# Late layernorms on VectorE, masks made ahead of layer 1, walk products ahead of the searches

## The chip, the cores and the metric

The kernel runs on one core of a Trainium2 chip. The metric is the device time of one execution in microseconds, as a median of several. The engines that matter are TensorE (PE in the profile: matrix products and transposes, into PSUM), VectorE (DVE), ScalarE (ACT), GpSimd (POOL) and the DMA queues; SyncE (SP) issues most of the transfers.

## What is computed

2708 nodes with 256 features go through two layers, each with a residual and a layernorm. All data is f32.

```
# layer 0, x: (2708, 256)
R = adj + I;  R = R / R.sum(-1)
Xf = Xa = x;  Z = 0
for n in range(2):
    A  = top_p_attention(Xa)      # softmax rows; the largest entries that make up 0.9, renormalised
    Xf = R @ Xf                   # the walk
    Xa = A @ Xa                   # the attention
    Z  = Z + Xf @ U1[n].T + Xa @ U2[n].T
x = layernorm(x + layernorm(x + Z) * ln_g + ln_b)
# layer 1, 4 heads of 64
Wh  = x @ W[h];  s_i, s_j = the two halves of a[h] with Wh
e   = leaky_relu(s_i + s_j, 0.2), masked by adj != 0 and the diagonal
out = layernorm(x + softmax_j(e) @ Wh)
```

## The kernel before

**Tiles.** The nodes are 22 row tiles, 16 of 128 rows and 6 of 110. Of PE, ACT, DVE and POOL each executes its instructions in the order in which the program is written (a manual schedule); so a line that stands earlier in the program goes earlier on each of its engines. Only SP's transfers are ordered by a scheduler.

**Layer 0** (fast_layer0) has two steps. In each step, row tile t needs a *search*, a *walk* and an *attention*. The search (L842) computes the row's scores on PE (the groups named lg, L661), exponentials on ACT (e, L665), tallies on ACT (junk, L686), and on DVE a bound (L751), the candidates (max8, L766), sorting and settling (L784 to L832) and the final masked row with its sum (L835). The attention turns e on PE (tr, L240), copies it to SBUF on ACT (eT, L245) and multiplies (att, L258); at its end ACT writes xa (L1030). The walk (walks, L855) is a stream of products, 22 a tile, of blocks of adj with the features; its PSUM tile has one buffer (ps_wk). When a tile's walk ends, DVE adds the tile itself (xf, L915, in step 0; xw, L974, in step 1), and only then may the next tile's walk begin.

A *slot* (L999) interleaves these. It advances the searches that are going by one part, may begin a new one, advances the work that finishes tiles, and then takes some walk products from the stream:

```
def slot(spend, begin=None):
    advance(going)
    if begin and begin[1] < NT:
        going.append(search(*begin)); next(going[-1])
    advance(doing)
    owed[0] += spend
    while owed[0] > 0:
        ...
```

Between the two steps there is no attention to interleave with: 15 slots of 7 walk products each run the first three searches of step 1 (L1117 to L1121). Within step 1, slots spend 6 or 7 products (SPEND_1).

**The end of layer 0.** finish (L969) adds up a tile, normalises it twice (norms, L181, layernorm on DVE with one power on POOL) and computes its *sources* (L156): two transposes of xe into PSUM (L160), a copy on ACT, two products with the layer's weights (L166), and from these the exponentials sb and tj and the values v, stored to DRAM. The last LATE = 4 tiles stop before the normalisation; their sums stay in x_late and they are normalised within layer 1.

**Layer 1** (L1193). The rows i are taken in three groups of 8, 8 and 6 tiles; for a group all 22 blocks j of neighbours are added up in PSUM. For block j the *mask* (neighbours, L1214) is loaded by SP into one of three buffers (blk) and turned to 0 and 1 by two passes of ACT, Sign and Square (L1221, L1222); where the block holds the diagonal DVE sets it (L1225). With the mask comes the load of v (L1290) in the first group, issued by ACT. The *weights* pt (L1302) are four operations of DVE, one a head: the larger of r and tj, times the mask. PE multiplies the *values* (L1313, 16 products a block) and the *denominators* (L1323, 16 a block). pt has three blocks' buffers (DEEP = 3). The main loop (from L1369) takes blocks in pairs: both blocks' values, then both blocks' denominators, then weights and masks of the blocks ahead. Twice a pair it calls *beside* (L1344), which advances other work by one part: the four late tiles (prepared, L1330) in group 0, the verdict (L1126; some 20 small operations of DVE that check that the searches held, and one product), and the settling of the group before (L1228).

prepared uses layernorm_beside (L138): ACT sums x (L145), POOL makes the mean (L146), ACT sums the squares (L148), POOL makes the variance, the power and the offset (L149 to L151), ACT writes the result (L153), and POOL multiplies by ln_g and adds x (L187, L188) between the two layernorms. The sources of the four late tiles are the last blocks of group 0.

**The tail** (from L1406). After the last group its six tiles are settled: PE transposes, DVE takes the reciprocal (L1236), ACT scales each head (L1247, even tiles) or DVE does all at once (L1242, odd tiles), POOL adds xe (L1252), DVE makes the statistics, POOL the power and the offset (L1262, L1263), ACT writes o (L1265; two buffers) and SP stores it.

Of the kernel before, what the change touches and what calls it, by code (L numbers as in the profile page):

```python
# [8 lines left out]
F32 = mybir.dt.float32  # L9
# [35 lines left out]
def kernel(  # L45
# [68 lines left out]
    g_sb = const.tile([P, D], F32, name="g_sb")  # L114
    b_sb = const.tile([P, D], F32, name="b_sb")

    LATE = 4
    x_late = const.tile([P, LATE, D], F32, name="x_late")
    engines = {nc.tensor.engine, nc.scalar.engine, nc.vector.engine, nc.gpsimd.engine}

# [57 lines left out]
            )  # L178
        queue.dma_start(vd[t][:m], vt[:m])  # L179

    def norms(t, xt, norm=layernorm, other=None):  # L181

        m = rows[t]
        hh = xe[:m, t, 0:D]
        h2 = hh if other is None else other()[:m]
        yield from norm(h2, hh, m)
        nc.gpsimd.tensor_mul(h2, h2, g_sb[:m])  # L187
        nc.gpsimd.tensor_add(h2, h2, xt[:m])  # L188
        yield
        yield from norm(hh, h2, m)  # L190
        yield
        if t < NT - LATE:
            yield

    GT = 8
    spans = [list(range(g, min(g + GT, NT))) for g in range(0, NT, GT)]
# [20 lines left out]
    def spread(g, r):  # L217

        lines = shared[g].rearrange("(t h) m -> h t m", h=H)
        n = len(spans[g]) * rows[spans[g][0]]  # L220
        for k in range(2):
            for h in range(2):
                nc.sync.dma_start(
                    r[k][:, h, :n].rearrange("p (t m) -> p t m", t=len(spans[g])),
                    lines[2 * k + h].partition_broadcast(P),
                )

    def room(pool):

# [295 lines left out]
    def fast_layer0(ep, adjp):  # L525
# [461 lines left out]


        going, doing, unfinished, stored = [], [], set(), set()
        ready, held = {}, {}  # L990
        stream = walks()
        owed = [0]
# [3 lines left out]
                if next(g, parts) is parts:  # L996
                    parts.remove(g)

        def slot(spend, begin=None):  # L999

            advance(going)
            if begin and begin[1] < NT:
                going.append(search(*begin))
                next(going[-1])
            advance(doing)
            owed[0] += spend
            while owed[0] > 0:
                owed[0] -= 1
                if next(stream, True):
                    break  # L1010

        def step(s, cur, spend):
            first = None
            for t in range(NT):
                m = rows[t]
                e, rden = ready[t]
                ac = ps_at.tile([P, CHUNK], F32, name="att")
                if s == 0 and t == NT - 1:
                    next(stream)
                if s and t == NT - 2:  # L1020
                    share(0, ps_tr.tile([P, 4, P], F32, name="tr"))
                if s and t == NT - 1:
                    ahead.extend(room(ep))
                    spread(0, ahead)

                def between(n):
                    last = n == len(groups) - 1
                    if last:
                        xa = heldp.tile([P, D], F32, name="xa1")
                        nc.scalar.activation(xa[:m], ac[:m, :D], AF.Copy, scale=rden)  # L1030
                        if s and t in c3:
                            nc.gpsimd.dma_start(c3[t][:m], xa[:m])
                            stored.add(t)
                        elif s:
                            held[t] = xa
                        else:
                            doing.append(after_attention0(t, xa))
                    slot(spend[n], (s, t + 3) if n == len(groups) - 2 else None)

                def turn_next(n):  # L1040
                    u = t + n // len(groups)
                    if u == NT:
                        return None
                    return turned(ready[u][0], rows[u], n % len(groups), tpp, ps_tr, nc.scalar.copy)

                first = weigh(
                    ac[:m, :D], first or turn_next(0), m,
                    lambda j: cur[: rows[j], j, 0:D], turn_next, between,
                )
                ready.pop(t)  # L1050
# [43 lines left out]
        with tc.manual_schedule(engines=engines):  # L1094
            query_weights()
            ahead = turn_x(groups[0])
            for n in range(len(groups)):
                c0, w = ahead
                if n + 1 < len(groups):
                    ahead = turn_x(groups[n + 1])  # L1100
                pj = ps_tr.tile([P, 4, P], F32, name="tr").rearrange("p a b -> p (a b)")
                project(
                    0, c0, w, pj, x_turned[:, :, c0 : c0 + w],
                    nc.scalar.copy, nc.vector.tensor_copy,
                )
            ahead = []
            for n in range(10):
                slot(0, (0, n // 4) if n in (0, 4, 9) else None)
                for t in range(n * NT // 10, (n + 1) * NT // 10):
                    terms1(t, x_turned[:, :, off[t] : off[t + 1]])  # L1110
            layer1_weights()
            step(0, xm, [0] * len(groups))
            while doing:
                slot(SPEND_BETWEEN)


            for t in range(3):  # L1117
                for n in range(6):
                    slot(SPEND_BETWEEN, None if n else (1, t))
                    if (t, n) == (2, 2):  # L1120
                        break  # L1121
            step(1, ba, SPEND_1)
            owed[0] = 0
            while doing:
                slot(NT)
# [56 lines left out]
            )  # L1182

        l0.close()
        return ahead, verdict

# [1 line left out]

    def layer1(ep, adjp, r=None, verdict=None):  # L1193
        l1 = ExitStack()

        pp, rp, pj, keep = (
# [7 lines left out]
        first = list(range(GT, NT - LATE)) + list(range(GT)) + list(range(NT - LATE, NT))  # L1204


        v = {}
        for t in reversed(first):
# [1 line left out]

        def aux():
            return ps_u.tile([P, H, P], F32, name="aux")

        def neighbours(g, j):  # L1214

            k = rows[j]
            i0, i1 = off[spans[g][0]], off[spans[g][-1] + 1]
            bar = adjp.tile([P, NT - HT, P], F32, name="blk")
            bar = bar.rearrange("p t d -> p (t d)")[:k, : i1 - i0]
            nc.sync.dma_start(bar, adjT[off[j] : off[j + 1], i0:i1])  # L1220
            nc.scalar.activation(bar, bar, AF.Sign)  # L1221
            nc.scalar.activation(bar, bar, AF.Square)  # L1222
            if j in spans[g]:
                own = bar[:, off[j] - i0 : off[j + 1] - i0]
                nc.vector.tensor_tensor(own, own, ident[:k, :k], op=ALU.max)  # L1225
            return bar

        def settle(g, t, val, den, u, last):  # L1228

# [8 lines left out]
            )  # L1238
            res = pp.tile([P, H, FO], F32, name="res", bufs=5)
            sums = u[:m, 0:2, :].rearrange("p q (h o) -> p (q h) o", h=2)  # L1240
            if last and t % 2:
                nc.vector.tensor_tensor(  # L1242
                    res[:m], sums, rden[:m].unsqueeze(2).to_broadcast([m, H, FO]), op=ALU.mult
                )
            else:
                for h in range(H):
                    nc.scalar.activation(  # L1247
                        res[:m, h, :], sums[:, h, :], AF.Copy, scale=rden[:m, h : h + 1]
                    )
            yield  # L1250
            flat = res[:m].rearrange("p h o -> p (h o)")
            nc.gpsimd.tensor_add(flat, flat, xe[:m, t, 0:D])  # L1252
            yield
            o = pp.tile([P, D], F32, name="o")[:m]
            if last:
# [30 lines left out]
        def mask(n):  # L1286
            if n < len(order):
                g, _, j = order[n]
                if g == 0:
                    nc.scalar.dma_start(  # L1290
                        v[j][: rows[j]].rearrange("p h o -> p (h o)"), vd[j][: rows[j]]
                    )
                masks[n] = neighbours(g, j)

        def weights(n):
            if n < len(order):
# [32 lines left out]

        def prepared(t):  # L1330

            yield from norms(
                t, x_late[:, t - NT + LATE, :], layernorm_beside,
                lambda: pp.tile([P, D], F32, name="h2", bufs=4),
            )
            yield from sources(t, pp, aux, nc.scalar)


        late = []
        if verdict:  # L1340
            late += [[2 * k, prepared(NT - LATE + k)] for k in range(LATE)]
            late.append([2 * LATE, verdict(aux)])
        rest, running = [], []
        def beside(g, i):  # L1344

            for part in list(late):
# [23 lines left out]
        for n in range(0, len(order), 2):  # L1370
# [13 lines left out]
            for u in (n, n + 1):  # L1384
                for k in range(2):
                    values(u, (2 * k, 2 * k + 1))
                    if last and u > n:
                        for c, (c0, w) in enumerate(cuts[g]):
                            copy = nc.scalar.copy if c == 0 else nc.vector.tensor_copy
                            copy(val[:, k, c0 : c0 + w], acc[k][c][:, :w])  # L1390
            for u in (n, n + 1):
                denominators(u)
            if last:
# [2 lines left out]
                    copy(den[:, c0 : c0 + w], acc[2][c][:, :w])  # L1396
                assert not rest
                rest = [(g, t, val, den) for t in spans[g]]
            else:
                beside(g, i + 1)  # L1400
            weights(n + 3)
            mask(n + 4)
        assert not late
# [70 lines left out]
```

## Time and profile before

| what | value |
|---|---|
| median of 3 executions | 1587.1 us (1586.86 to 1587.92) |
| the profiled execution | 1586.25 us, its span 1584.4 us |
| mean granted clock of PE | 0.993 |
| busy: PE, DVE, ACT, POOL | 97%, 76%, 50%, 28% of the span |
| values L1313, denominators L1323 | 213.7 and 106.8 us of PE |
| weights pt, L1302 | 185.5 + 109.8 us of DVE |
| last attention product ends | 1221.1 us |
| group 0 of layer 1 ends | 1359.7 us |
| last o of the tail starts | 1573.69 us |

A line of a timeline holds the start in us, the length, the engine, the line of the program, the operation with its output and inputs by the program's names, the shapes, how many instructions in a row it covers, and in brackets how long the engine was idle before and which instruction ended that. A line of the waits names who waited for whom, with the sum, the number and the longest. A line of the windows holds for each engine its busy time in that stretch and, at the end, the granted clock of PE (1.00 is full), the DMA share and GB/s.

### The profile page before, as it was taken

To read this page: it belongs to the slowest core of one execution; us is meant where nothing else is said; L and a number is where in the kernel's file an instruction comes from. 1 tells how busy PE (TensorE), PEld (TensorE's weight loads), DVE (VectorE), ACT (ScalarE), POOL (GpSimd) and SP (SyncE) were. 2 spreads that over 40 slices of the span, in tenths; PEclk is the share of its full clock that TensorE was granted. 3 is DMA by queue.
4 is the path that set the end of the run, shared out by engine and by line. 5 is a ranking of instruction groups with operands and counts; after the bars stand their busy time and mean duration, and the time that the engine had idled before them with its cause. 6 is when DMAs were issued, how large, how long until landed. Compare 5 with 4: busy or idle time off the path is not lost. (4 is left out here: it accounts for less than half of the span.)

```text
span 1584.4 us, 23826 instructions
## 1 busy us (share of the span) xinstructions
PE 1537.4 (97%) x8029; PEld 1036.2 (65%) x8029; DVE 1201.2 (76%) x3651; ACT 799.5 (50%) x1462; POOL 440.9 (28%) x884
## 2 busy tenths in 40 slices
PE   8999999999998999999999999999998989999994
PEld 4477777776776888787778788887786323333342
DVE  4686776777309767877779888888883888999895
ACT  3444444444345455555645566656643454456473
POOL 2200000100023122232223544444541750044133
PEclk9999999999999999999999999999999999999998
DMA  6100000000144333332333444333343335334231
GB/s 163 61 12 13 9 13 9 9 11 11 43 114 105 100 84 102 80 89 72 85 89 95 110 109 109 104 99 93 91 101 110 110 110 161 95 107 133 81 100 43
DMA packets 172495, 128.27 MB, mean 81 GB/s; under 512 B 44342, under 2 KB 161804, under 8 KB 172362
## 3 DMA queue, kind: packets, MB, share of 16 engines
q1 hardware_dynamic: 162000, 111.86, 26.4%
q0 software_dynamic: 3648, 9.26, 1.7%
q10 hardware_dynamic: 6714, 5.54, 1.1%
q8 instruction: 65, 1.06, 0.3%
q14 instruction: 68, 0.56, 0.1%
HBM read 111.78 MB, written 13.46 MB: 79 GB/s over the span
## 5 line engine op out<-in xcount | busy, mean ns | idle before, releaser
L245 ACT COPY eT<-tr 128x512 f32<-128x512 f32 (+5 forms) x264 | 141.3, 535 | 287.5 <-PE tr L240 284.9
L686 ACT ACTIVATE junk<-e,minus,rth 128x2708 bf16<-128x2708 f32 (+1 forms) x88 | 232.8, 2646 | 36.1 <-POOL rth L718 35.2
L258 PE MATMUL att<-xm,eT 128*128 128x256 f32 (+3 forms) x968 | 230.9, 380 | 0.4 <-ACT xa L1030 0.4
L258 PE MATMUL att<-ba,eT 128*128 128x256 f32 (+3 forms) x968 | 230.8, 379 | 0.3 <-ACT eT L245 0.2
L901 PE MATMUL walk<-xe,blk 128*128 128x257 f32 (+3 forms) x968 | 225.3, 384 | 5.0 <-DVE xf L915 5.0
L901 PE MATMUL walk<-xm,blk 128*128 128x256 f32 (+3 forms) x968 | 222.0, 380 | 1.0 <-DVE xw L974 1.0
L1313 PE MATMUL acc<-pt,v 128*64 128x512 f32 (+3 forms) x1056 | 213.7, 548 | 4.5 <-DVE pt L1302 4.1
L901 PEld LDWEIGHTS walk<-xe,blk 128*128 128x128 f32 (+3 forms) x968 | 178.5, 187 | 50.3 <-issue 12.6
L1302 DVE SCALAR_TENSOR_TENSOR pt<-e,tj,blk 128x1024 f32<-128x1024 f32 (+3 forms) x176 | 185.5, 1122 | 20.7 <-ACT blk L1222 16.0
L901 PEld LDWEIGHTS walk<-xm,blk 128*128 128x128 f32 (+3 forms) x968 | 177.7, 186 | 34.4 <-issue 4.9
L258 PEld LDWEIGHTS att<-xm,eT 128*128 128x128 f32 (+3 forms) x968 | 169.6, 186 | 22.1 <-ACT xa L1030 0.8
L258 PEld LDWEIGHTS att<-ba,eT 128*128 128x128 f32 (+3 forms) x968 | 169.5, 186 | 22.0 <-ACT eT L245 0.8
L665 ACT ACTIVATE e<-lg 128x1024 f32<-128x1024 f32 (+1 forms) x132 | 121.0, 921 | 110.6 <-PE lg L661 107.0
L1313 PEld LDWEIGHTS acc<-pt,v 128*64 128x64 f32 (+1 forms) x1056 | 74.7, 137 | 132.9 <-issue 109.4
L766 DVE MAX8 cand<-e 128x8 f32<-128x170 f32 (+1 forms) x352 | 89.6, 324 | 90.5 <-ACT e L665 90.4
L240 PEld LDWEIGHTS tr<-ident,e 128*128 128x128 f32 (+3 forms) x968 | 115.1, 138 | 56.3 <-issue 21.0
L240 PE MATMUL tr<-ident,e 128*128 128x128 f32 (+3 forms) x968 | 147.1, 271 | 0.7 <-ACT xe L952 0.3
L1302 DVE SCALAR_TENSOR_TENSOR pt<-r,tj,blk 128x1024 f32<-128x1024 f32 (+1 forms) x88 | 109.8, 1312 | 6.1 <-PE acc L1323 3.2
L1323 PE MATMUL acc<-pt,sb 128*32 128x512 f32 (+3 forms) x1056 | 106.8, 545 | 0.0
L766 DVE MAX8 cand<-scr 128x8 f32<-128x97 f32 (+1 forms) x616 | 102.3, 246 | 0.0
L915 DVE TENSOR_TENSOR xf<-walk,xe 128x257 f32<-128x257 f32 (+1 forms) x22 | 9.4, 426 | 110.6 <-PE walk L901 110.6
L784 DVE MAX8 top<-work 128x8 f32<-128x128 f32 (+3 forms) x242 | 82.4, 340 | 8.3
(237 smaller groups left out, 1966.9 us busy)
## 6 DMA issues: line engine op xcount, KB each, us to landing
blk<-in_adjT_dram SPq DMA_DIRECT2D x32, 704.0 KB
blk<-in_adjT_dram SPq DMA_DIRECT2D x32, 512.0 KB
blk<-in_adjT_dram SPq DMA_DIRECT2D x48, 330.0 KB
blk<-in_adjT_dram SPq DMA_DIRECT2D x32, 320.0 KB
blk<-in_adjT_dram SPq DMA_DIRECT2D x12, 605.0 KB
blk<-in_adjT_dram SPq DMA_DIRECT2D x12, 440.0 KB
blk<-in_adjT_dram SPq DMA_DIRECT2D x18, 283.6 KB
c<-cs POOLq DMA_DIRECT2D x32, 128.0 KB, 2.0
```

The source lines that it names most:

```text
L240: nc.tensor.transpose(tr[: rows[t], q, :m], e[:m, off[t] : off[t + 1]], ident[:m, :m])
L245: copy(eT[:k, : len(grp), :m], tr[:k, : len(grp), :m])
L258: nc.tensor.matmul(acc, eT[: rows[t], q, :m], value(t), start=(t == 0), stop=(t == NT - 1),)
L665: nc.scalar.activation(halves[:m, :, c0 : c0 + w], lg[:m, :, :w], AF.Exp, accum_out=zp[:m, n : n + 1],)
L686: nc.scalar.activation(junk[:m], e[:m], func, scale=rth, bias=minus1[:m], accum_out=acc)
L766: nc.vector.max(cand[:, n, :], src[:m, n * size : min(N, (n + 1) * size)])
L784: nc.vector.max(top[:, k : k + 8], work if k else flat)
L901: nc.tensor.matmul(ac[:m, :w], blk[: rows[j], j - j0, :m], cur[: rows[j], j, 0:w], start=(j == 0), stop=(j == NT - 1),)
L915: nc.vector.tensor_add(xf[:m], ac[:m, : D + 1], xe[:m, t, :])
L1302: nc.vector.scalar_tensor_tensor(pt[:k, :gw], targets[g][h // 2][:k, h % 2, :gw], tj[:k, j, h : h + 1], bar, op0=ALU.max, op1=ALU.mult,)
L1313: nc.tensor.matmul(acc[h // 2][c][q * FO : (q + 1) * FO, :w], v[j][:k, h, :], probs[n][h][:k, c0 : c0 + w], **at,)
L1323: nc.tensor.matmul(acc[2][c][h * 32 : (h + 1) * 32, :w], sb[:k, j, h : h + 1].to_broadcast([k, 32]), probs[n][h][:k, c0 : c0 + w], **at,)
```

## The change

- LATE is 3: tile 18 is normalised and projected at the end of layer 0, three tiles stay for layer 1.
- The masks of the first two blocks of layer 1 (early) are loaded and made within step 1 of layer 0, at the last but one slot of its last attention.
- In the slots between the steps the 7 walk products are written ahead of the search parts. In all other slots the order stays.
- prepared no longer uses layernorm_beside. Statistics (bn_stats, bn_aggr), epsilon and offset are on DVE, the power on POOL, the result on ACT; the multiplication by ln_g and the addition of x are on DVE. Three parts of beside lie between the power and the offset.
- The verdict begins 26 calls of beside late instead of 8, so in group 1.
- The second beside of a pair is written ahead of the pair's denominators instead of behind them.
- The first three loads of v are issued by SP instead of ACT.
- In the tail the odd tiles' four heads are scaled and added to xe by four operations of DVE; POOL's addition is left for the even tiles alone.

```diff
-    LATE = 4
+    LATE = 3
...
-        if t < NT - LATE:
-            yield
+        yield
...
-        def slot(spend, begin=None):
-
-            advance(going)
-            if begin and begin[1] < NT:
-                going.append(search(*begin))
-                next(going[-1])
-            advance(doing)
+        def slot(spend, begin=None, walk_first=False):
+
+            def search_parts():
+                advance(going)
+                if begin and begin[1] < NT:
+                    going.append(search(*begin))
+                    next(going[-1])
+                advance(doing)
+
+            if not walk_first:
+                search_parts()
             owed[0] += spend
             while owed[0] > 0:
                 owed[0] -= 1
                 if next(stream, True):
                     break
+            if walk_first:
+                search_parts()
...
+                    if s and (t, n) == (NT - 1, len(groups) - 2):
+
+                        early.extend(neighbours(0, j, adjp) for j in first[:2])
                     slot(spend[n], (s, t + 3) if n == len(groups) - 2 else None)
...
-                    slot(SPEND_BETWEEN, None if n else (1, t))
+                    slot(SPEND_BETWEEN, None if n else (1, t), True)
...
             if last and t % 2:
-                nc.vector.tensor_tensor(
-                    res[:m], sums, rden[:m].unsqueeze(2).to_broadcast([m, H, FO]), op=ALU.mult
-                )
+                for h in range(H):
+                    nc.vector.scalar_tensor_tensor(
+                        res[:m, h, :], sums[:, h, :], rden[:m, h : h + 1],
+                        xe[:m, t, h * FO : (h + 1) * FO], op0=ALU.mult, op1=ALU.add,
+                    )
...
-            nc.gpsimd.tensor_add(flat, flat, xe[:m, t, 0:D])
+            if not (last and t % 2):
+                nc.gpsimd.tensor_add(flat, flat, xe[:m, t, 0:D])
...
-                    nc.scalar.dma_start(
+                    (nc.sync if n < DEEP else nc.scalar).dma_start(
                         v[j][: rows[j]].rearrange("p h o -> p (h o)"), vd[j][: rows[j]]
                     )
-                masks[n] = neighbours(g, j)
+                masks[n] = early[n] if n < len(early) else neighbours(g, j, adjp)
...
         def prepared(t):
 
-            yield from norms(
-                t, x_late[:, t - NT + LATE, :], layernorm_beside,
-                lambda: pp.tile([P, D], F32, name="h2", bufs=4),
-            )
+            m = rows[t]
+            xt = x_late[:m, t - NT + LATE, :]
+            hh = xe[:m, t, 0:D]
+            h2 = pp.tile([P, D], F32, name="h2", bufs=LATE)[:m]
+            for src, dst in ((hh, h2), (h2, hh)):
+                if src is h2:
+                    nc.vector.tensor_mul(h2, h2, g_sb[:m])
+                    nc.vector.tensor_add(h2, h2, xt)
...
+                nc.vector.bn_stats(st, src)
+                nc.vector.bn_aggr(mv, st)
+                nc.vector.tensor_scalar(ve, mv[:, 1:2], LN_EPS, None, op0=ALU.add)
+                nc.gpsimd.tensor_tensor(rs, ve, minus_half[:m], op=ALU.pow)
+
+                yield
+                yield
+                yield
+                nc.vector.tensor_scalar(nb, mv[:, 0:1], rs, -1.0, op0=ALU.mult, op1=ALU.mult)
+                yield
+                nc.scalar.activation(dst, src, AF.Identity, scale=rs, bias=nb)
+                yield
             yield from sources(t, pp, aux, nc.scalar)
...
-            late.append([2 * LATE, verdict(aux)])
+            late.append([NT + 4, verdict(aux)])
...
+            if not last:
+                beside(g, i + 1)
             for u in (n, n + 1):
                 denominators(u)
...
-            else:
-                beside(g, i + 1)
```

The function neighbours moves out of layer1 unchanged (it is given the pool of blk), and so does the list first, the order of the blocks of group 0.

More of the change, by code (lines that the diff above doesn't have):

```diff
@@ L179, in sources, with norms @@
         queue.dma_start(vd[t][:m], vt[:m])
-    def norms(t, xt, norm=layernorm, other=None):
+    def norms(t, xt):
         m = rows[t]
         hh = xe[:m, t, 0:D]
[L185 to L188, printed above, removed]
+        yield from layernorm(hh, hh, m)
+        nc.gpsimd.tensor_mul(hh, hh, g_sb[:m])
+        nc.gpsimd.tensor_add(hh, hh, xt[:m])
         yield
-        yield from norm(hh, h2, m)
+        yield from layernorm(hh, hh, m)
         yield
-        if t < NT - LATE:
-            yield
+        yield
     GT = 8
@@ L226, in spread, with neighbours @@
                 )
+    first = list(range(GT, NT - LATE)) + list(range(GT)) + list(range(NT - LATE, NT))
+    def neighbours(g, j, adjp):
+        k = rows[j]
+        i0, i1 = off[spans[g][0]], off[spans[g][-1] + 1]
+        bar = adjp.tile([P, NT - HT, P], F32, name="blk")
+        bar = bar.rearrange("p t d -> p (t d)")[:k, : i1 - i0]
+        nc.sync.dma_start(bar, adjT[off[j] : off[j + 1], i0:i1])
+        nc.scalar.activation(bar, bar, AF.Sign)
+        nc.scalar.activation(bar, bar, AF.Square)
+        if j in spans[g]:
+            own = bar[:, off[j] - i0 : off[j + 1] - i0]
+            nc.vector.tensor_tensor(own, own, ident[:k, :k], op=ALU.max)
+        return bar
     def room(pool):
@@ L989, in fast_layer0 @@
         going, doing, unfinished, stored = [], [], set(), set()
+        early = []
         ready, held = {}, {}
@@ L1010, in slot @@
                     break
+            if walk_first:
+                search_parts()
         def step(s, cur, spend):
-            first = None
+            turned_first = None
             for t in range(NT):
@@ L1044, in turn_next @@
                     return turned(ready[u][0], rows[u], n % len(groups), tpp, ps_tr, nc.scalar.copy)
-                first = weigh(
-                    ac[:m, :D], first or turn_next(0), m,
+                turned_first = weigh(
+                    ac[:m, :D], turned_first or turn_next(0), m,
                     lambda j: cur[: rows[j], j, 0:D], turn_next, between,
@@ L1184, in fast_layer0, with layer1 @@
         l0.close()
-        return ahead, verdict
-    def layer1(ep, adjp, r=None, verdict=None):
+        return ahead, verdict, early
+    def layer1(ep, adjp, r=None, verdict=None, early=()):
         l1 = ExitStack()
@@ L1202, in layer1 @@
         ps_v = l1.enter_context(tc.tile_pool(name="ps_v", bufs=1, space=PSUM))
-        first = list(range(GT, NT - LATE)) + list(range(GT)) + list(range(NT - LATE, NT))
         v = {}
@@ L1212, in aux @@
             return ps_u.tile([P, H, P], F32, name="aux")
[L1214 to L1226, printed above, removed]
         def settle(g, t, val, den, u, last):
@@ L1240, in settle @@
             sums = u[:m, 0:2, :].rearrange("p q (h o) -> p (q h) o", h=2)
+            flat = res[:m].rearrange("p h o -> p (h o)")
             if last and t % 2:
-                nc.vector.tensor_tensor(
-                    res[:m], sums, rden[:m].unsqueeze(2).to_broadcast([m, H, FO]), op=ALU.mult
-                )
+                for h in range(H):
[3 more added lines that the diff above has]
+                    )
             else:
@@ L1250, in settle @@
             yield
-            flat = res[:m].rearrange("p h o -> p (h o)")
-            nc.gpsimd.tensor_add(flat, flat, xe[:m, t, 0:D])
+            if not (last and t % 2):
+                nc.gpsimd.tensor_add(flat, flat, xe[:m, t, 0:D])
             yield
@@ L1330, in prepared @@
         def prepared(t):
-            yield from norms(
-                t, x_late[:, t - NT + LATE, :], layernorm_beside,
-                lambda: pp.tile([P, D], F32, name="h2", bufs=4),
-            )
+            m = rows[t]
[6 more added lines that the diff above has]
+                    nc.vector.tensor_add(h2, h2, xt)
+                st = small.tile([P, 6], F32, name="ln_st")[:m]
+                mv = small.tile([P, 2], F32, name="ln_mv")[:m]
+                ve, rs, nb = (small.tile([P, 1], F32, name=f"ln_{k}")[:m] for k in ("ve", "rs", "nb"))
+                nc.vector.bn_stats(st, src)
[9 more added lines that the diff above has]
+                yield
             yield from sources(t, pp, aux, nc.scalar)
```

## The prediction

> **What bounds the kernel now.** I read the page first: engine shares, then the chain that ended last.
>
> ```profile
> PE 1537.4 (97%) x8029; PEld 1036.2 (65%) x8029; DVE 1201.2 (76%) x3651; ACT 799.5 (50%) x1462; POOL 440.9 (28%) x884
> ```
>
> TensorE (PE) is busy 97% of the span, so the time can fall only where PE waits, runs on a lower clock, or has less to do. The windows view shows where that is.
>
> ```profile
> 1200.00:1230.00 30.00, 25.89 (x127) 19.20 (x126) 9.16 (x10) 11.19 (x18) 4.67 (x7) 0.94 0.31 90
> 1260.00:1320.00 60.00, 53.49 (x321) 17.60 (x315) 52.51 (x64) 30.51 (x74) 28.42 (x27) 1.00 0.48 140
> 1320.00:1560.00 240.00, 240.00 (x1679) 85.09 (x1679) 223.38 (x241) 132.99 (x253) 60.17 (x80) 1.00 0.35 101
> ```
>
> The first number is PE's busy time, the last but two the granted clock. From 1320 us on PE never pauses; all slack of layer 1 lies in its start and in the late layernorms of group 0. The waits of PE and its timeline name the places.
>
> ```profile
> PE aux L160 <- ACT xe L153: 6.5, 3, 2.2
> PE walk L901 <- DVE xf L915: 5.0, 3, 3.2
> ...
> PE acc L1313 <- DVE pt L1302: 4.1, 1, 4.1
> ```
>
> ```profile
> 506.70 8.90 PE L901 MATMUL walk<-xe,blk 128*128 128x257 f32 x32 [3.18 <-DVE xf L915]
> ...
> 523.33 3.21 PE L901 MATMUL walk<-xe,blk 128*128 128x257 f32 x14
> ```
>
> ```profile
> 1218.35 2.75 PE L258 MATMUL att<-ba,eT 110*110 110x256 f32 x12
> 1225.22 10.30 PE L1313 MATMUL acc<-pt,v 128*64 128x512 f32 x32 [4.11 <-DVE pt L1302]
> 1235.45 3.64 PE L1323 MATMUL acc<-pt,sb 128*32 128x512 f32 x32
> 1239.02 7.09 PE L1313 MATMUL acc<-pt,v 128*64 128x512 f32 x32
> 1246.04 3.64 PE L1323 MATMUL acc<-pt,sb 128*32 128x512 f32 x32
> 1249.61 9.21 PE L1313 MATMUL acc<-pt,v 128*64 128x512 f32 x32
> ```
>
> An undisturbed pair of blocks is 7.02 of values and 3.57 of denominators, 10.59 us. Pair 1 takes 3.28 more (the clock is 0.50 in 1225 to 1228, after the 4.11 us pause), pair 3 takes 2.19 more (its weights come late). Group 0, from T = 1221.1 (last attention product) to 1359.7, thus adds up: 4.1 pause, 11 x 10.59 = 116.5, 3.28, 2.19, three L160 waits 6.5, four late tiles' auxiliary products at 0.34 + 1.09 = 5.7, the share 0.3: 138.6. That is the measured length.
>
> **The change part by part.** Orders named here are those of the changed program's instructions on each engine.
>
> *Walk before search (between the steps).* The wait of 3.18 us, and the half clock behind it (508.5 to 510.5 at 0.50; 32 records in 8.90 us where 44 took 9.83, so 1.75 lost), look like 5 us to win. The three xf (L915) now stand on VectorE (DVE) ahead of the bound, the candidates and the match that held them, so PE's waits become some 0.5 + 0.5 + 1.95 for 0.5 + 1.31 + 3.18, and PE reaches the first transpose of step 1 4.1 us earlier. But the third score piece of a search now stands behind 13 walk products; that search and DVE's unbroken chain behind it come 5.1 us later. The fourth xf, which had this slack, loses it:
>
> ```profile
> 521.43 0.43 DVE L915 TENSOR_TENSOR xf<-walk,xe 128x257 f32<-128x257 f32 x1 [3.81 <-PE walk L901]
> ```
>
> It would end at 523.1, and since the walk has one PSUM buffer the next tile's walk starts at 523.15, against 523.33 above. The gain is handed to a new wait: I take 0.2 gain; bounds 4.1 (DVE catches up) and -1.5 (a turned tile, eT, comes late behind a tally on ScalarE (ACT) and the delay stays).
>
> *Three late tiles for four.* Tile 18's two products go into layer 0: 0.19 + 0.89 = +1.1 at their pitch there. DVE's 2.4 us of its layernorms fall into a pause of 4.08 at 1195.2 (DVE waits for the walk): 0. If that cover is gone, the last search and the end of layer 0 slip by up to 2.4. In layer 1 it takes 1.43 off.
>
> *Early masks.* Now all three masks (2.1 each) follow the last xa on ACT:
>
> ```profile
> 1223.88 24.01 DVE L1302 SCALAR_TENSOR_TENSOR pt<-e,tj,blk 128x1024 f32<-128x1024 f32 x20 [11.34 <-ACT blk L1222]
> ```
>
> In the changed order the masks of blocks 0 and 1 stand among the last eT copies; mask 0 is ready at T - 0.05, mask 1 at T + 2.05, xa at T + 2.5, and 8 pt (1.20 each) begin at T + 0.1 for T + 2.75. The mask's DMA on the SP queue moved 512 KB in 2 us (1213.0 to 1215.0), and there is no other transfer ahead of it that is wanted earlier. The first values product then waits for xa, not pt: its PSUM is that of the attention. T + 2.5 for 4.11: -1.6. A pause of 2.5 lies between one of 2.2, after which the clock stays 1.00 (1262 to 1317), and one of 3.18, after which it was 0.50; I take full clock. Pair 1 is then fed by pt: 0.1 + 9.7 + the last products and 3.57 end it at T + 14.6, 1.5 over undisturbed, -1.8. Pair 3's 2.19 go as well, since DVE keeps its lead. [...]
>
> *First v loads on SP.* The v load issued at 1221.15 moved 1222.0 to 1223.0. Issued by SP after the last attention it lands near T + 1.9, ahead of xa: 0; up to +1 if later.
>
> *Late layernorms on DVE.* GpSimd (POOL) was the chain: one small operation of it lasted as long as DVE's run of pt:
>
> ```profile
> 1234.98 12.96 POOL L149 TENSOR_SCALAR lb_sq<-lb_sq 110x1 f32<-110x1 f32 x1 [6.13 <-ACT h L148]
> ```
>
> It ended at 1247.94, DVE's run at 1247.9. With BN 0.43, AGG 0.18, VE 0.15 on DVE and only the power left on POOL, xe is ready before its transposes: -6.5 of L160 waits. In exchange DVE does 6 x (0.43 + 0.18 + 0.15 + 0.15) + 3 x 2 x 0.42 = 8.0 us more in the first six pairs, where a pair gives it 10.59 and pt takes 9.7 to 10.6. Followed pair by pair PE waits 1.2 + 0.7 + 0.3 + 0.4 = 2.6 (bounds 0 and 9). Behind each nb that waits for the power stand pt, and PE behind them; three steps lie between, some 1.5 pairs. [...]
>
> *Verdict later, auxiliary products ahead of the denominators.* 3.9 us of DVE move to group 1, over 3.5 pairs with about 0.8 free each and a block of lead: 0 (bound +1.5). The order costs PE nothing itself.
>
> Group 0: -1.6 - 1.8 - 2.2 - 6.5 - 1.4 + 2.6 = -10.9.
>
> *Tail.* POOL loses three additions of 0.68, but o has two buffers and each o waits for an output transfer of some 2 us; second, fourth and sixth o in a chain end at 1573.45 for 1573.69. I take -0.2 (bounds 0 and -1).
>
> Sum: -0.2 + 1.1 - 10.9 - 0.2 = -10.2. The profiled execution took 1586.25 (span 1584.4), so 1576.0; the median shown is 0.85 above it: **1576.9**.
>
> **Rivals.** (a) *More is kept.* DVE catches up between the steps, or group 0 has no new stall: 2 to 6 more, 1571 to 1575. For it: DVE had waits of 3.81 and 1.80 soon after 521. Against: its rows from 479 to 517 have no gap.
> (b) *DVE becomes the bound of group 0.* 88 pt at 1.32 (as in 1267.92, 10.59 for 8, beside POOL) are 116.2; with 2.4 for diagonals, 8.0, and six waits for the power at 0.9, 132 for 138.6: -6.6 + 0.7 = -5.9, 1581; up to 1584 at 1.36. For it the 5.34 us for 4 at 1280.93; against it the 4.87 of most later rows.
> (c) *Slower.* The same place and mechanism, with pt at 1.45 beside POOL's operations (5.82 for 4 at 1261.53): 127.6 + 15.8 = 143.4, 4.8 more than 138.6; with the other parts +5.5, 1592.6. It decides from a pitch of (138.6 - 15.8) / 88 = 1.40. Against: POOL has 6 powers there for some 50 operations before.
> (d) *The changed order gives the wait back.* For the walk this is in the forecast.
>
> **How the numbers follow.** About 0.2% (3.2 us) is what a measurement of this kernel can tell from no change. Forecast (1575 to 1580) 0.48; (a) 0.20; (b) 0.18; little moves (1584 to 1590) 0.08; (c) 0.06. Faster is the first three less what of (b) lies above 1583.9: 0.85; same 0.09; slower 0.06. The range 1571 to 1584.5 reaches from (a) through (b); only (c), most of "little moves" and the ends of (a) are outside.
>
> **What would show it.** Right: the first acc (L1313, L1325 after the change) waits 2.5 us or less, for xa, and the clock stays 1.00; no 2.2 us waits of L160; pair 1's values take 8.5; pt at 1.20 to 1.25; walk waits of 0.5, 0.5 and 2, and a new wait of the walk on xf early in step 1; the six o within 0.5 of their old distance from the den copy. Wrong: a mask or v that lands after T + 2, the half clock at the start of layer 1, DVE without a pause over all of group 0, or the first tile of step 1 as early as 511 with its successors also 4 us early.

## The result and the profile after

The changed kernel took 1577.26 us (median of 4 executions, 1574.76 to 1578.42), the kernel before 1587.34 beside it (1586.86 to 1587.92): ratio 0.9934, 95% interval 0.9917 to 0.9951. The forecast was 1576.9. The profiled execution took 1577.32 with a span of 1575.5. The total was foretold within 0.4 us, but several of its terms were wrong, in opposite directions, and the largest term had the wrong cause.

The page of the kernel after, and its windows over the same stretches as before:

```profile
PE 1538.2 (98%) x8029; PEld 1037.9 (66%) x8029; DVE 1208.2 (77%) x3698; ACT 792.3 (50%) x1428; POOL 414.6 (26%) x850
```

```profile
1200.00:1230.00 30.00, 27.49 (x134) 20.85 (x133) 10.72 (x14) 11.79 (x24) 6.00 (x7) 0.95 0.36 101
1260.00:1320.00 60.00, 59.97 (x347) 19.64 (x343) 56.40 (x69) 28.67 (x51) 8.26 (x3) 1.00 0.49 144
```

PE has the same work. From 1260 to 1320 its busy time went from 53.49 to 59.97, and no wait of L160 is left among the waits of PE. Behind a load of 4.9 at the program's start (4.8 before), the list begins:

```profile
PE att L273 <- ACT eT L260: 3.8, 1, 3.8
PE acc L1325 <- DMA v<-v: 2.5, 1, 2.5
PE walk L916 <- DVE xf L930: 2.3, 3, 1.3
```

The wait on xf fell from 5.0 to 2.3, and a new one of 3.8 is now the longest within the layers: the first attention of step 1 waits for its turned tile (eT). PE's timeline between the steps, after:

```profile
502.57 4.18 PE L916 MATMUL walk<-xe,blk 128*128 128x257 f32 x18 [1.28 <-DVE xf L930]
...
510.58 1.04 PE L255 MATMUL tr<-ident,e 128*128 128x128 f32 x8
515.38 3.78 PE L273 MATMUL att<-ba,eT 128*128 128x256 f32 x8 [3.76 <-ACT eT L260]
```

PE reaches the transposes at 510.58 (before 515.45), waits, and then the 8 products take 3.78 instead of 1.99. The window over them shows why:

```profile
515.00:519.00 4.00, 3.62 (x9) 2.91 (x10) 3.73 (x17) 3.45 (x4) 1.18 (x5) 0.50 0.00 0
```

The clock is 0.50 behind the pause. PE's timeline at the start of layer 1, after (T, the end of the last attention product, is 1224.05; the values of pair 1 are the first line of L1325, and so on):

```profile
1221.30 2.75 PE L273 MATMUL att<-ba,eT 110*110 110x256 f32 x12
1226.57 10.16 PE L1325 MATMUL acc<-pt,v 128*64 128x512 f32 x32 [2.51 <-DMA v<-v]
1236.66 3.64 PE L1335 MATMUL acc<-pt,sb 128*32 128x512 f32 x32
1240.23 7.09 PE L1325 MATMUL acc<-pt,v 128*64 128x512 f32 x32
1247.24 3.64 PE L1335 MATMUL acc<-pt,sb 128*32 128x512 f32 x32
1250.82 7.09 PE L1325 MATMUL acc<-pt,v 128*64 128x512 f32 x32
...
1261.40 8.18 PE L1325 MATMUL acc<-pt,v 128*64 128x512 f32 x32
...
1273.09 7.85 PE L1325 MATMUL acc<-pt,v 110*64 110x512 f32 x32
...
1284.44 0.41 PE L160 MATMUL aux<-ident,xe 110*128 110x110 f32 x2
```

The pause is 2.51 (forecast 2.5), pair 3 has lost its excess (9.21 to 7.09), pairs 4 and 5 are longer by 1.09 and 0.76 (DVE is late), and the transposes of xe no longer wait.

By stage, profiled execution against profiled execution, each end read from PE's timelines (the last product is the last of L1323, after the change L1335):

| stage | forecast | measured |
|---|---|---|
| to the end of layer 0 (1221.11 to 1224.05) | +0.9 | +2.9 |
| group 0 (138.6 to 128.95) | -10.9 | -9.6 |
| groups 1 and 2 (202.2 to 202.5) | 0 | +0.3 |
| last product to the end of the span (22.5 to 20.1) | -0.2 | -2.4 |
| sum | -10.2 | -8.8 |

The first stage holds 0.5 us that no edit made: the last attention product of step 0, ahead of all that differs, ended at 440.88 before and at 440.39 after. In the fourteen profiles of this document it ended between 439.2 and 440.9. So below, stages are counted from that product where it matters.

### The profile page after: what moved, and what is told of

Its sections match the earlier page's. It is cut to its first block, busy times and chain, and to the rows that moved or that the text cites. A ratio compares the mean times of both kernels' runs of the same rounds, so it can differ in the third digit from the quotient of the medians.

```text
span 1575.5 us, 23768 instructions
## 1 busy us (share of the span) xinstructions
PE 1538.2 (98%) x8029; PEld 1037.9 (66%) x8029; DVE 1208.2 (77%) x3698; ACT 792.3 (50%) x1428; POOL 414.6 (26%) x850
## 4 chain that ended last, share of the span: by engine, by line
PE 92%; DVE 4%; ACT 1%; POOL 1%; issue 1%; DMA 0%; ACTq 0%; POOLq 0%; DVEq 0%
PE att L273 25%; PE walk L916 25%; PE acc L1325 13%; PE lg L676 7%; PE acc L1335 7%; PE tr L255 6%; PE tr L961 2%; PE tr L975 2%; PE tr L646 1%; PE tr L166 1%; DVE pt L1314 1%; ACT junk L701 1%; DVE scr L847 0%; DVE scr L766 0%; PE aux L1242 0%
## 5 line engine op out<-in xcount | busy, mean ns | idle before, releaser
L1325 PE MATMUL acc<-pt,v 128*64 128x512 f32 (+3 forms) x1056 | 214.2, 549 | 2.7 <-DMA v<-v 2.5
L1325 PEld LDWEIGHTS acc<-pt,v 128*64 128x64 f32 (+1 forms) x1056 | 75.8, 137 | 131.9 <-issue 107.7
L1335 PE MATMUL acc<-pt,sb 128*32 128x512 f32 (+3 forms) x1056 | 106.8, 545 | 0.0
L236 ACT ACTIVATE blk<-blk 128x1024 f32<-128x1024 f32 (+3 forms) x66 | 63.3, 959 | 80.8 <-DMA blk<-in_adjT_dram 69.3
```

Source lines behind the costliest of these rows:

```text
L1325: nc.tensor.matmul(acc[h // 2][c][q * FO : (q + 1) * FO, :w], v[j][:k, h, :], probs[n][h][:k, c0 : c0 + w], **at,)
L1335: nc.tensor.matmul(acc[2][c][h * 32 : (h + 1) * 32, :w], sb[:k, j, h : h + 1].to_broadcast([k, 32]), probs[n][h][:k, c0 : c0 + w], **at,)
```

## The experiments

Ratios are to the kernel before on the same chip, with 95% intervals. With four executions an interval reaches some 0.17%, or 2.6 us, to each side, so it doesn't tell kernels apart that differ by little more.

**1. The walk order alone.** Edit: only slot(..., True) and its new body.

> The kernel before with the walk products ahead of the search parts between the steps, nothing else. Theory (the gain is given back): the walk's three waits on xf shrink from 5.0 to about 2.3 us, but the first attention of step 1 waits some 3.8 us for its turned tile behind a tally on ACT, and the half clock follows; ratio 1.000 to 1.001 (0 to +1.5 us). Rival (the removed waits are kept, and the whole change owes part of its gain to them): 3 to 5 us faster, 0.997 to 0.998.

Measured 1589.07 (1586.56 to 1590.76), 1.0011 (1.0001 to 1.0021): not faster. The ten executions fall into two heaps, four at 1586.6 to 1586.9 with a mean clock of 0.991 to 0.993 and six at 1589.0 to 1590.8 with 0.989 to 0.990. The profiled one is of the first heap; its timeline and clock:

```profile
515.02 1.99 PE L258 MATMUL att<-ba,eT 128*128 128x256 f32 x8 [3.75 <-ACT eT L245]
```

```profile
514.00:517.00 3.00, 1.98 (x9) 1.78 (x10) 2.86 (x15) 3.00 (x5) 0.92 (x3) 1.00 0.00 0
```

The same pause of 3.75 us here left the clock at 1.00. From the last attention product of step 0 to the first transposes of tile 1 in step 1 this profile takes 99.9 us for 100.4 before, so the new order keeps 0.5 where no half clock follows the pause. In the changed kernel, where the clock is 0.50 for 6.8 us, the same stretch takes 102.2; in run 7, with 3.4 us of it, 101.2. What the second heap lost wasn't profiled; its lower mean clock fits such spells.

**2. The layernorms alone.** Edit: the new prepared, and the verdict at NT + 4; LATE stays 4.

> The kernel before with the late layernorms (all four) on DVE and the verdict moved to group 1, nothing else. Theory (POOL's chain made the 6.5 us of L160 waits): these waits are gone, the late start of the weights stays; 4 to 7 us faster, 0.9956 to 0.9975. Rival (DVE becomes the bound of group 0, since it has 10.7 us more there): new waits of PE on pt eat most of it; 0 to 2 us faster.

Measured 1586.25 (1584.74 to 1589.06), 0.9999 (0.9990 to 1.0009). Neither saw all of what happened: the L160 waits are all still there, with DVE doing the statistics.

```profile
PE aux L160 <- ACT xe L1353: 6.5, 3, 2.2
```

This refutes the forecast's reason for -6.5. The timelines of ACT and PE in the kernel before show the real one:

```profile
1273.25 1.14 PE L166 MATMUL aux<-wx,xT 128*110 128x264 f32 x4
1276.58 0.41 PE L160 MATMUL aux<-ident,xe 110*128 110x110 f32 x2 [2.19 <-ACT xe L153]
```

```profile
1274.43 0.17 ACT L170 ACTIVATE sb<-aux 110x4 f32<-110x4 f32 x1 [2.10 <-PE aux L166]
...
1274.63 0.93 ACT L176 ACTIVATE cs<-aux,sb 110x64 f32<-110x64 f32 x4
...
1275.93 0.60 ACT L153 ACTIVATE xe<-h,lb_nb,lb_rs 110x256 f32<-110x256 f32 x1 [0.37 <-ACT cs L176]
```

The last call of beside in a pair puts one tile's products L166 on PE, and on ACT first the seven results of these, with the issue of their store, and then the next tile's xe. The first call of the next pair puts that tile's transposes L160 directly behind L166. So PE waits for ACT to do seven operations and xe: 2.2 us, whoever made the statistics. In this run too xe begins right behind cs, 0.39 us after it.

The zero is a sum. In the profile layer 1 is 3.7 us longer than before (the values of pairs 4 to 6 take 8.18, 8.60 and 8.10 for 7.09, as the rival said DVE would cause; pair 3 loses its 2.1; a half clock behind the last L160 wait takes 1.7; groups 1 and 2 take 0.6 more), and the end of the program 2.4 shorter (20.1 for 22.5), of which more below.

**3. The early masks alone.** Edit: early, and the first v loads on SP.

> The kernel before with the first two masks made ahead of layer 1 and the first v loads on SP, nothing else. Theory (the weights begin earlier): the pause at the start of layer 1 falls from 4.1 to 2.5 us and pair 3 loses its 2.2 us; 3 to 4 us faster, 0.9975 to 0.998. Rival (the late layernorms' chain is what sets the length of group 0, so an earlier start only makes the L160 waits longer): 0 to 1 us faster.

Measured 1583.33 (1582.19 to 1585.48), 0.9977 (0.9967 to 0.9987). The theory holds: the pause is 2.22 and pair 3 takes 7.09; the three L160 waits stay. Behind the second of them the clock was 0.50 (from 1287.6 to 1290.9), which it was behind none of them in the kernel before, and pair 6 takes 8.78 for 7.09:

```profile
1286.09 0.41 PE L160 MATMUL aux<-ident,xe 110*128 110x110 f32 x2 [2.21 <-ACT xe L153]
1286.42 8.78 PE L1318 MATMUL acc<-pt,v 128*64 128x512 f32 x32
```

**4. The tail alone.** Edit: the four operations of DVE for the odd tiles.

> The kernel before with the odd tiles of the tail added on DVE, nothing else. Theory of the forecast (o's two buffers and its output transfers set the end): 0.2 us faster, bounds 0 and 1. Rival (the program's end is POOL's closing drain of 6.7 us, which begins when POOL's last operation of the tail is done, so three additions less on POOL count): 0.9 us faster, and up to 2.4 if the 2.9 us between POOL's last branch and its drain shrink to 1.4 as in the changed kernel.

Measured 1586.28 (1585.07 to 1587.32), 0.9994 (0.9985 to 1.0004): a gain of 0.8, not told from none by its interval. In the profile POOL's last operation ends 10.68 us after the last product of group 2 for 11.72, and the span 21.23 for 22.51, while the last o starts at the same distance (11.78 for 11.83). That speaks for the rival; run 9 tests it.

**5. The auxiliary call ahead of the denominators, alone.**

```diff
+            if not last:
+                beside(g, i + 1)
             for u in (n, n + 1):
                 denominators(u)
...
-            else:
-                beside(g, i + 1)
```

> The kernel before with the pair's second auxiliary call written ahead of the denominators, nothing else. New theory (the three L160 waits of 2.2 us are the latency from ACT's xe to a transpose that stands right behind it on PE, since the last call of a pair and the first of the next follow one another; 3.6 us of denominators between them cover it): the 6.5 us of waits vanish, 6 to 8 us faster, 0.995 to 0.996. Rival, the step of the forecast (POOL's slow chain makes xe late, and the order of the calls costs nothing itself): 0 to 1 us faster, the waits stay.

Measured 1579.79 (1579.53 to 1580.64), 0.9958 (0.9941 to 0.9974): 7.2 us faster, by one call in a new place. In the profile group 0 is 5.3 shorter: 6.5 of waits are gone, and in pair 9 a wait of DVE for a mask costs 1.4 (8.54 for 7.09). PE's timeline shows the cover, the denominators between L166 and the next L160, which has no wait:

```profile
1268.64 1.14 PE L166 MATMUL aux<-wx,xT 128*110 128x264 f32 x4
1269.71 3.64 PE L1323 MATMUL acc<-pt,sb 128*32 128x512 f32 x32
1273.33 0.41 PE L160 MATMUL aux<-ident,xe 110*128 110x110 f32 x2
```

**6. The changed kernel with the old place of that call.**

> The changed kernel with the pair's second auxiliary call back behind the denominators. New theory: two or three L160 waits of about 2.2 us are back (4.4 to 6.6 us) and perhaps a half clock behind one of them; 4 to 8 us slower than the changed kernel, so 1581 to 1585. Rival, the forecast (the layernorms on DVE took the waits away): no slower than the changed kernel, 1577.

Measured 1582.88 (1582.23 to 1584.12), 0.9976 (0.9967 to 0.9986), 5.6 over the changed kernel; group 0 takes 133.7 for 128.95. Two waits are back with the layernorms on DVE:

```profile
PE aux L160 <- ACT xe L1365: 2.4, 1, 2.4
...
PE aux L160 <- DMA blk<-in_adjT_dram: 2.2, 1, 2.2
```

The second is put down to a mask's transfer, but ACT's xe, again right behind cs, ends just before these transposes as well (1314.28, the transposes begin at 1314.33).

**7. The changed kernel with the old layernorms.**

> The changed kernel with the late layernorms as they were (ACT's sums, POOL's small operations and its two long ones) for the three late tiles. New theory (not the engine but the place of the call mattered): 1576 to 1579, within 2 us of the changed kernel, since DVE then has 8 us less in group 0 and POOL's slowness has cover. Rival, the forecast: the waits on xe come back, 4 to 6 us slower than the changed kernel, 1581 to 1583.

Measured 1573.10 (1572.29 to 1575.93), 0.9919 (0.9902 to 0.9935): 4.2 below the changed kernel in the medians, though their intervals overlap. POOL's slow chain has cover, and DVE is no longer late in pairs 4 and 5:

```profile
1259.90 7.09 PE L1327 MATMUL acc<-pt,v 128*64 128x512 f32 x32
...
1271.90 7.09 PE L1327 MATMUL acc<-pt,v 110*64 110x512 f32 x32
```

Group 0 takes 127.45 for 128.95. These 1.5 us are what the layernorms account for: in the four profiles that have them and the new place of the call (the changed kernel, runs 8, 9 and 10) group 0 takes 128.93 to 128.95, in the three with the old ones and otherwise the same layer 1 (runs 7, 11 and 12) 127.15 to 127.87. The rest of the difference lies ahead of the change (0.9), between the steps, where the half clock lasted 3.4 us for 6.8 (0.9), and in the end of the program (19.0 behind the last product for 20.1).

**8. The changed kernel with the old walk order.**

> The changed kernel with the search parts ahead of the walk products between the steps, as before. Theory (the new order costs 1.7 us by itself, as the walk-alone run had it): 1 to 2.5 us faster than the changed kernel, 1574.8 to 1576.3. Rival, the forecast (0.2 us gained by the new order): equal to the changed kernel or slower, 1577 to 1578.

Measured 1574.90 (1573.28 to 1575.03), 0.9926 (0.9909 to 0.9943): 2.4 below the changed kernel, with overlapping intervals. In its profile layer 0 ends at 1221.13 for 1224.05, while group 0 takes the same 128.93. Of these 2.9 us, 1.2 lie ahead of the change and 1.9 between the steps (100.3 for 102.2); the end of the program is 1.1 shorter here too (18.98 for 20.07).

**9. Six buffers of o.** Edit: o has bufs=6 in the tail.

> The changed kernel with six buffers of o in the tail, so that no o waits for an output transfer. Theory (POOL's drain of 6.7 us, begun behind its last operation of the tail, sets the end): the last o starts 1.4 us earlier, the span's end does not move; equal to the changed kernel within 0.3 us by the profile's tail. Rival, the forecast (the chain of o and its transfers sets the end): 1.4 us less between the last products and the end of the span.

Measured 1576.48 (1575.04 to 1578.21), 0.9933 (0.9916 to 0.9949). ACT's last line and POOL's drain, first in the changed kernel, then here:

```profile
1567.72 0.60 ACT L1277 ACTIVATE o<-res,ln_nb,ln_rs 110x256 f32<-110x256 f32 x1 [1.78 <-DMA out_dram<-o]
```

```profile
L1502 POOLq DRAIN  x3: 40/107/6685, 1568.0 to 1575.3; - x3
```

```profile
1566.28 0.60 ACT L1277 ACTIVATE o<-res,ln_nb,ln_rs 110x256 f32<-110x256 f32 x1 [0.45 <-POOL ln_nb L1275]
```

```profile
L1502 POOLq DRAIN  x3: 40/107/6685, 1567.8 to 1575.1; - x3
```

The wait of 1.78 is gone and the last o starts 1.4 earlier, but POOL's drain of 6.685 us (the third of the three numbers) begins at 1567.8 for 1568.0, and the span ends at 1575.3 for 1575.5. So the drain sets the end, and the chain of o doesn't.

**10. A mixed walk order.** Edit: `slot(SPEND_BETWEEN, None if n else (1, t), n != 1)`, so a search's two score pieces stand together.

> The changed kernel, but in the second slot of a search the search part goes first again, so that a search's two score pieces stand together on PE and the xf still stand ahead of the bound and the match on DVE. Theory (the new order lost because the third score piece came 13 walk products later, which pushed the tally in front of the first turned tile): the 3.8 us wait for eT and its half clock shrink or vanish while the waits on xf stay short; 4 to 6 us faster than the changed kernel, 1571 to 1573. Rival (DVE's unbroken chain of searches is the bound between the steps, and whatever PE gains there it gives back in a wait on the fourth xf): 1575 to 1577.

Measured 1576.74 (1576.09 to 1578.30), 0.9934 (0.9917 to 0.9950). My theory of the late score piece fell: the piece now comes 4.1 us earlier on ACT, and the wait for eT grew. The rival's number fits, but its wait on the fourth xf isn't there (two waits on xf, 0.5 each).

```profile
PE att L273 <- ACT eT L260: 4.4, 1, 4.4
```

POOL and DVE in this run show another cause:

```profile
503.73 3.65 POOL L933 TENSOR_SCALAR xf<-xf,rinv 128x256 f32<-128x256 f32 x1 [9.02 <-DVE rinv L931]
...
508.69 2.93 POOL L690 TENSOR_SCALAR tau<-fact 128x1 f32<-128x1 f32 x1
```

```profile
503.54 3.02 DVE L850 SCALAR_TENSOR_TENSOR e<-scr,fact,e 128x2708 f32<-128x2708 f32 x1
...
508.49 3.04 DVE L766 SCALAR_TENSOR_TENSOR scr<-e,hi 128x2708 f32<-128x2708 f32 x1
```

POOL's xf, 0.94 us in the kernel before, takes 3.65, and tau, 0.23 before, takes 2.93: the second ends with DVE's operation of 3 us, the first 0.8 behind it. The earlier xf puts POOL's work inside DVE's two long operations, of 3.02 and 3.04, and the tally on ACT, which needs POOL's numbers, comes late. The changed kernel has the like beside the same two operations (3.64 for xf, 2.17 for the operation ahead of tau). Why POOL's operations last so long there isn't shown. That this made the tally late is read from the traces; a kernel that takes POOL out of there was not tried.

**11. Both undone.** Edit: 7 and 8 together.

> The changed kernel with the walk order and the late layernorms both as before (so three late tiles, early masks, the auxiliary call ahead of the denominators, the later verdict, v on SP and the tail remain). Theory (the two are losses in different places and add up): 2.4 + 4.2 us faster than the changed kernel, 1570 to 1572. Rival (they share one loss, the half clock behind a pause): 1573, no better than the better of the two alone.

Measured 1574.13 (1573.68 to 1574.71), 0.9920 (0.9903 to 0.9936). The sum of the two gains is not reached in the medians. Counted in the profiles from the last attention product of step 0 to the end of the span, the changed kernel takes 1135.2 us, run 7 1131.6, run 8 1132.3 and this one 1131.0: gains of 3.6 and 2.9 alone and 4.2 together. Part of the two is the same: each ends the program 1.1 us sooner, and 0.9 of run 7's lies between the steps, where the old order takes its place. The rest adds up. Differences of about 1 us between the medians of runs 7, 8 and 11 are within the spread of the part ahead of them.

**12. All that looked good, together.** Edit: 7, 9, 10, and the tail's nb on DVE.

> The changed kernel with the mixed walk order, the late layernorms as before, six buffers of o and the tail's offset nb made on DVE instead of POOL. Theory: what the mixed order gains and what the old layernorms gain add up, and POOL's last operation of the tail comes 0.3 to 1 us earlier, so the end does; 1566 to 1569. Rival (the gains between the steps are given back, see the mixed order alone): 1571 to 1573.

Measured 1578.16 (1577.63 to 1579.87), 0.9947 (0.9931 to 0.9964): 0.9 above the changed kernel in the medians, not told from it, and far from the 1566 to 1569 expected. The mixed order gains little, as in run 10, and nb on DVE makes the tail longer: DVE stops for each power and holds back the next tile.

```profile
1560.06 0.21 DVE L1277 TENSOR_SCALAR ln_nb<-ln_mv,ln_rs 110x1 f32<-110x1 f32 x1 [0.66 <-POOL ln_rs L1276]
```

POOL's last operation ends 14.56 us after the last product for 10.86, and the span 22.6 for 20.1. This edit was expected to gain and cost 2.6 us.

## Why the prediction was right, and where it was wrong

- **Walk before search (-0.2 forecast).** Right that the gain is handed to a new wait, and right in naming eT behind a tally as the way to lose; wrong in the main path (the fourth xf stands on DVE 0.82 before its walk ends, so it holds nothing). The half clock behind the new wait was the term put at nothing: from the last attention product of step 0 to the first transposes of tile 1 it is +1.75 here (102.2 for 100.4) and -0.5 in run 1, where no half clock followed the new wait.
- **Three late tiles (+1.1).** From there to the end of layer 0 it takes 1.7 more. This is firm: 679.8 to 680.0 in the five profiles with four late tiles, 681.5 to 681.7 in the nine with three. 1.1 is the products, and the walk's waits on xw are 1.3 for 1.0 in all; the last 0.3 stays open.
- **Early masks (-1.6 and -2.2).** Right in both, with an experiment of their own. But by the profile the first product here waits for the first v load, not for xa, which ends at T + 2.23. In the five profiles where ACT issues its first v load at T, beside those of SP, the pause is 2.5 to 2.8; in the four where ACT's comes 3.2 later it is 2.2 to 2.3.
- **Pair 1 (-1.8).** Wrong: 10.16 for 10.30. The half clock, which the forecast named as a sign of being wrong, came behind the pause of 2.51, but it isn't what holds the pair: run 11 had none there, and in all nine profiles with early masks pair 1 ends 16.2 us behind T, with pauses of 2.2 to 2.8. What holds it is pt. The first 8 take 10.60, not 9.7, since two of them take 1.75 beside POOL's two additions for the last late tile; and from the eighth to the end of the values it is 2.0, where the sum left 1.2.

```profile
1224.15 10.60 DVE L1314 SCALAR_TENSOR_TENSOR pt<-e,tj,blk 128x1024 f32<-128x1024 f32 x8 [8.66 <-PE att L273]
```

```profile
1226.43 0.79 POOL L996 TENSOR_TENSOR xe<-xe,xa 110x256 f32<-110x256 f32 x1 [9.26 <-ACT xa L1052]
1227.17 1.71 POOL L997 TENSOR_TENSOR x_late<-x_late,b_sb 110x256 f32<-110x256 f32 x1
```

- **Late layernorms (-6.5, and 2.6 of new stalls).** The 6.5 were gained, for another reason: the step that said POOL's chain made xe late, and "the order costs PE nothing itself", failed. The order alone gave 7.2 in the medians and 5.3 in group 0 of its profile; DVE's layernorms alone left all three waits. The stalls were right: 1.09, 0.76 and 0.62 in pairs 4 to 6, 2.5 in sum. So this part of the change costs; run 7 puts it at 1.5, since without the new layernorms DVE waits for a mask in pair 9 instead (8.06 for 7.09). No wait of DVE for a power shows in group 0 of the changed kernel, where the six powers take POOL 1.46 to 5.23 us; the 0.9 us that rival (b) gave each such wait was an estimate, which this profile doesn't show.
- **Verdict.** Forecast 0; groups 1 and 2 are 0.3 longer.
- **Tail (-0.2).** Wrong: 2.4 less from the last product to the end. I let the chain of o set the end and took the 10 us behind it as fixed. In all profiles the end lies 0.8 to 1.1 us behind POOL's drain, and this begins when POOL's last operation and some code behind it are done. Here POOL ends 0.86 sooner, and the time from there to the drain is 1.69 for 3.27. In the five profiles with the verdict in its old place that time is 2.9 to 3.5, in the nine with the later verdict 0.6 to 1.8; the later verdict is the only edit that all nine share (run 2 has 0.79 with the old tail). It was not moved alone, so it isn't shown to be the cause, and how it would act is open. The drain in the kernel before:

```profile
L1470 POOLq DRAIN  x3: 40/107/6685, 1576.9 to 1584.1; - x3
```

The errors of +2.0, +1.3, +0.3 and -2.2 come to +1.4. Of this 0.85 doesn't show, since the forecast added as much for the median over the profiled execution, and in the changed kernel the two are alike (1577.26 and 1577.32). So the hit within 0.4 is in good part luck. The size of the gain in group 0 was foreseen; its cause, and the shares of the other parts, were not.

## What to carry to other kernels

A wait has three parts, the waiter, the one waited for, and the place where both were written: before speeding up the releaser, look what stands in front of it on its own engine, and whether a block of the waiter's independent work can be moved between. Do one part of a combined change alone and undo it alone; here the part with the most new code cost time, and one call in a new place gave most of the gain. The lowest median, 1573.10 in run 7, has the change without its layernorms; runs 8 and 11 are not told from it.

## What the runs showed of the hardware

The clock dropped to 0.50 behind pauses of 2.51 and 3.76 us in the changed kernel, and stayed at 1.00 behind one of 3.75 in run 1. Behind the L160 waits of 2.1 to 2.2 us it stayed at 1.00 in the kernel before, but dropped behind one of the three in each of runs 1 to 3 (2.10, 2.22 and 2.21), where the values that follow take 8.78 for 7.09. Behind the same pause of 2.28 at the start of layer 1 it dropped in run 7 and not in run 11 (1.00 from 1225 to 1232). So the length of a pause alone doesn't tell whether PE slows, and a forecast can't take 2.2 us as safe from one profile. Between the steps and at the start of layer 1 the drops lasted 3.41 and 3.41 us in the kernel before, 6.83 and 3.41 in the changed kernel; what decides whether one comes, and how long it lasts, isn't shown.

Beside DVE's operations of 3.02 and 3.04 us an operation of POOL took 3.65 us in run 10 for 0.94 in the kernel before, and another 2.93 for 0.23.

POOL's closing drain took 6.685 us in the profiles before and after, and set the end of the span in each, 0.8 us behind it.
